# Storing the transposed blocks of x once, in the preparation, and loading them back in layer 1's stage

## The chip, the core and the metric

The kernel runs on one core of a Trainium2 chip. The metric is the device time of one execution in microseconds (us). A core has TensorE (PE in the profile; PEld is its weight load), VectorE (DVE), ScalarE (ACT), GpSimd (POOL) and SyncE (SP, which here only issues transfers). Each engine carries out its own instructions in order; semaphores hold one engine back for another. Transfers run on 16 DMA engines which the queues of SP, ACT and POOL share.

## What is computed

Two layers of a relational graph attention network on 3125 nodes with 768 features and 53125 edges of three relations, then a residual and a layernorm:

```python
xr = jnp.einsum('nd,rdf->rnf', x, W)
oi = xr[etype, dst]; oj = xr[etype, src]
alpha = jax.nn.leaky_relu(oi @ q + oj @ k, NEG_SLOPE)
e = jnp.exp(alpha - segment_max(alpha, dst)[dst])
a = e / (segment_sum(e, dst)[dst] + EPS)
out = segment_sum(a[:, :, None] * oj.reshape(...), dst) + b
...
h = jax.nn.elu(rgat_conv(x, W1, q1, k1, b1, ...))      # 4 heads
out = rgat_conv(h, W2, q2, k2, b2, ...)                # 1 head
return _layernorm(x + out)
```

## The kernel before, in words

Nodes are taken in 25 blocks of 128 rows (the last has 53), features in 6 pieces of 128. Every float32 product is made of three in a reduced form (fp32r): a matrix is split into a high and a low part, and high·high, high·low and low·high are summed. TensorE multiplies along the partitions, so a block of x must be transposed, 6 pieces of 128x128, before it can be multiplied by W. The order of all instructions is written out by hand; nothing is rescheduled. Four stages follow one another.

**The preparation** (to about 120 us). `weights_kq` folds the weights of the queries and keys, `nodes_kq` then makes every node's query and key values. It goes over x two blocks a step, m = 1 to 12, and the single block 0 ahead of them. `Buffers` (`go`, L189) loads x into seven shared tiles, a new block whenever one is freed; one of the seven is lent to the rows of block 0 most of the time, so six turn over. Each `turn(m)` makes 12 transposes (`transposes`, L271) into three PSUM tiles `pt0` to `pt2` with two buffers each, frees the two tiles of x at once, brings the result of two steps ago into place (`place`, L379, L381), and splits the transposed data (`split_parts`: ScalarE copies the high part, L281; VectorE subtracts, L282). Then TensorE does a piece of block 0's own rows (`first`, L403, which ScalarE copies out, L410), and `product(m-1)` (L293), whose result ScalarE copies out of the one PSUM tile `bank` (`sm`, L370) for the next steps. In `weights_kq` L321 is the same kind of copy.

**Layer 1's keys' stage**, `phase1` (about 120 to 655 us): 144 groups of 18 products (`d_group`, L724) make the feature rows of blocks 1 to 24 for three relations, six groups to a block; ScalarE copies each result to one of three row tiles (L743) and SP stores it to the table `tab1` (L745). A list of events by group number n holds all the rest: VectorE's work on edges and softmax, a few small products, and, six groups apart, a block of x: `x_load` brings block b into the tile `xr` (L524), `d_turn(b)` at n = 6b-8 transposes it again (L701) into PSUM `px`, `d_split(b)` at n = 6b-7 splits it to `xT` (L708 on ScalarE, L709 on VectorE), adds the bias b2 to the untransposed block (L711) and stores the sum in `xb_d` (L712), from which the last stage takes its residual. POOL gathers one key vector for each edge by indirect transfers (L479 into `kt`), and every sixth product waits for a certain one of them ("an even load"), so that gathers and products go side by side. W2 is split beside this and, in the last groups, loaded by ScalarE's queue over the parts of wH and wL that are no longer needed (L532).

**Layer 2's features**, `phase2` (to about 1396 us): POOL gathers rows of `tab1` (L479 into `share` and `g`); VectorE makes selection matrices (`selp`, L471); TensorE sums (L978) and multiplies by W2 (L1055). Its first gather waits until all rows of `tab1` are stored. **The last stage** sums layer 2's rows (L1260), adds `xb_d` and normalizes.

Transfers of one queue are carried out in their order. SP's queue holds the loads of x, the row stores, the stores of `xb_d` and the edge data; an instruction of SP that waits holds back all behind it.

Of the kernel before, what the change touches and what calls it, by code (L numbers as in the profile page):

```python
# [8 lines left out]
F32 = mybir.dt.float32  # L9
# [11 lines left out]
P = 128  # L21
# [39 lines left out]
def kernel(  # L61
# [48 lines left out]
    tab2 = dram.tile([(N + P) * R, RW], F32, name="ftab2")  # L110
    kt1 = dram.tile([NP * R, 4], F32, name="kt1")
    xb_d = dram.tile([NP + P, D], F32, name="xb_d")
# [235 lines left out]
    def nodes_kq(buf, pre, work, psum, bank, wk, kqs, wH, wL, qq, more, edges_ready):  # L348
# [7 lines left out]
        def turn(m):  # L356
            b, nb = chunk(m)
            pts = transposes(psum, [buf["x", b + c] for c in range(nb)])
            for c in range(nb):
                buf.free("x", b + c)  # L360
            if m > 1:
                place(m - 2, prod.pop(m - 2))
            return split_parts(work, pts, nb * P, "t" if m else "t0")

# [137 lines left out]
    xs = {}  # L502
# [16 lines left out]
    def x_load(pre, b, to=None):  # L519
        n = min(P, N - b * P)  # L520
        xs[b] = pre.tile([P, D], F32, name="xr", bufs=1) if to is None else to[:, :D]
        if n < P:
            V.memset(xs[b], 0.0)
        nc.sync.dma_start(xs[b][:n], x[b * P:b * P + n, :])  # L524

# [12 lines left out]
    def phase1(pre, work, psum, wH, wL, qq):  # L538
# [7 lines left out]
        st = a_st  # L546
# [143 lines left out]
        xt = {}  # L690
        b2r = share[5][:, :D]
# [3 lines left out]

        def d_turn(b):
            xr = xs.pop(b)
            xt[b] = work.tile([P, 2, DT, P], F32R, **spare.get(b, dict(name="xT", bufs=2)))
            pt = psum.tile([P, 2, 512], F32, name="px", bufs=1)
            for t in range(DT):  # L700
                T.transpose(pt[:, t // 3, (t % 3) * P:(t % 3 + 1) * P], xr[:, t * P:(t + 1) * P], ident)  # L701
            p3 = pt[:, :, :3 * P]
            st["x", b] = xr, p3

        def d_split(b):
# [77 lines left out]
        nc.sync.dma_start(q1_d[NP:, :], als[0].rearrange("p j h -> p (j h)")[:, :H1 * R * 3 // 2].bitcast(BF))  # L783
        d_turn(1)
        d_split(1)
# [18 lines left out]
        GB = NB - 4  # L804
# [17 lines left out]
        for b in range(NB - LATE, NB):  # L822
            n = 6 * b + 2
# [18 lines left out]
        for b in range(2, GB + 1):  # L842
            for d, f, o in ((-8, d_turn, 0), (-7, d_split, 0), (-7, x_next, 1)):
                ev.setdefault(6 * b + d, []).append((f, NB - 1 if f is x_next and b == GB else b + o))
        last_w2 = second_weights(R - 1, wH, wL)
        for n in range(max(ev) + 1):
            for f, b in ev.get(n, ()):
                f(b)
            b, i = divmod(n, 6)
            if n == 2:  # L850
                nc.sync.dma_start(share[3][:, :D], x[:P, :])
            if n == 8:
                V.tensor_add(share[4][:, :D], share[3][:, :D], b2r)
                nc.sync.dma_start(xb_d[:P, :], share[4][:, :D])
            m = n - 6 * (GB - 1)
            if m in (1, 3, 5):
                d_turn(GB + 1 + m // 2)
                d_split(GB + 1 + m // 2)
# [1149 lines left out]
```

## Time and profile before

| what | value |
|---|---|
| three runs | 1985.41, 1987.32, 1988.5 us; median 1987.32 |
| the profiled execution | 1984.63 us, of it 1982.8 us span |
| preparation, layer 1's stage, layer 2's features, last stage (about) | 120, 535, 740, 585 us |
| PE busy over the span | 1680.7 us (85%) |
| POOL, DVE, ACT busy | 1333.2, 1201.9, 376.5 us |
| transposes of the preparation, L271 | 258 |
| transposes of layer 1's stage, L701 | 144 |
| chain that ended last | PE 60%, issue 10%, POOL 8%, DMA 7%, DVE 5% |

The page's chain follows the work that ended last back from the last instruction; its shares say which engine set the end. "Idle before, releaser" is the time that an engine had nothing to do, and what ended it. In a timeline a row is start, duration, engine, line, operation, output<-input and, in brackets, the idle time ahead of it. A row of the windows gives busy time and instruction count of each engine in a stretch, the granted clock of TensorE, the busy share of the DMA engines and GB/s.

### The profile page before, as it was taken

What the parts mean: (1) busy time and instruction counts of PE and PEld (TensorE: products, weight loads), DVE (VectorE), ACT (ScalarE), POOL (GpSimd) and SP (SyncE); (2) the same over time, 40 slices, a digit from 0 to 9 for tenths busy, and PEclk for the clock granted to TensorE, in tenths of its full rate; (3) what the DMA queues carried; (4) which work ended last, traced back from release to release, by engine and by line L of the source; (5) the groups of instructions that cost most, each with busy time, mean ns of one, the idle gap of its engine ahead of it and who ended that gap; (6) DMA issues with size and microseconds to landing.
All of it is one profiled execution on the core that took longest, in us unless ns stands there. A gap on an engine that the chain in (4) does not pass through costs nothing.

```text
span 1982.8 us, 41452 instructions
## 1 busy us (share of the span) xinstructions
PE 1680.7 (85%) x14727; PEld 1406.6 (71%) x14727; DVE 1201.9 (61%) x4296; ACT 376.5 (19%) x661; POOL 1333.2 (67%) x1326
## 2 busy tenths in 40 slices
PE   6989999999999599999999999999465556556664
PEld 6979999999999489898989999899222223223322
DVE  6544555555554667767776777774456665666564
ACT  5421222221221011111111111111011211121111
POOL 4247777777771467777777776652577777777773
PEclk8989999999999899999999999999677777777777
DMA  7556545554557988888888888886799999999994
GB/s 196 191 122 189 179 162 187 170 167 159 182 186 242 365 274 272 294 271 278 272 297 268 276 273 297 271 277 215 252 322 334 331 334 347 335 318 317 327 321 145
DMA packets 161018, 506.48 MB, mean 255 GB/s; under 512 B 47925, under 2 KB 61244, under 8 KB 160803
## 3 DMA queue, kind: packets, MB, share of 16 engines
q0 software_dynamic: 81904, 331.52, 50.6%
q1 hardware_dynamic: 67101, 156.21, 22.3%
q10 hardware_dynamic: 11798, 16.00, 2.5%
q8 instruction: 120, 1.97, 0.4%
q14 instruction: 95, 0.78, 0.1%
HBM read 412.74 MB, written 95.69 MB: 256 GB/s over the span
## 4 chain that ended last, share of the span: by engine, by line
PE 60%; issue 10%; POOL 8%; DMA 7%; DVE 5%; ACT 1%; POOLq 0%; DVEq 0%; ACTq 0%; SPq 0%
PE po L1055 25%; PE po L724 20%; PE acc L978 10%; POOL G L479 8%; DMA G<-ftab,ridx 6%; PE acc L1260 2%; PE pt L1030 1%; DVE selp L471 1%; PE px L701 1%; PE acc L1272 1%; DVE share L674 0%; DVE F L1219 0%; DMA share<-ftab,rfirst 0%; DVE share L675 0%; DVE sT L624 0%
## 5 line engine op out<-in xcount | busy, mean ns | idle before, releaser
L1055 PE MATMUL po<-wH,hT 128*128 128x386 f32 (+1 forms) x1800 | 485.0, 344 | 3.1 <-DVE hT L1043 2.2
L479 POOL DMA_INDIRECT kt<-kt,ridx x374 | 397.4, 1062 | 113.9 <-issue 106.6
L479 POOL DMA_INDIRECT G<-ftab,ridx x374 | 376.2, 1006 | 113.9 <-issue 99.3
L724 PE MATMUL po<-wH,xT 128*128 128x384 f32 x1584 | 435.7, 346 | 5.5 <-ACT share L743 2.4
L471 DVE TENSOR_SCALAR selp<-frow,fdl,pall 128x32 f32<-128x32 f32 (+1 forms) x1688 | 384.0, 321 | 0.7 <-PE acc L978 0.7
L1055 PEld LDWEIGHTS po<-wH,hT 128*128 128x128 f32 x1800 | 330.5, 189 | 18.8 <-issue 14.7
L479 POOL DMA_INDIRECT share<-ftab,ridx x239 | 239.2, 1001 | 100.7 <-PE acc L978 47.4
L1055 PE MATMUL po<-wL,hT 128*128 128x386 f32 (+1 forms) x900 | 305.6, 340 | 0.0
L724 PEld LDWEIGHTS po<-wH,xT 128*128 128x128 f32 x1584 | 292.9, 190 | 9.3 <-ACT share L743 4.2
L724 PE MATMUL po<-wL,xT 128*128 128x384 f32 x792 | 269.5, 340 | 0.0
L1260 PE MATMUL acc<-G,selp 128*32 128x386 f32 x2292 | 249.2, 584 | 6.6 <-DVE selp L471 6.6
L1260 PEld LDWEIGHTS acc<-G,selp 128*32 128x32 f32 x2292 | 126.8, 128 | 102.7 <-issue 53.7
L479 POOL DMA_INDIRECT g<-ftab,ridx x135 | 135.2, 1001 | 64.5 <-PE acc L978 34.0
L978 PE MATMUL acc<-share,selp 128*32 128x193 f32 x3088 | 165.7, 330 | 13.5 <-DVE selp L471 11.1
L1063 ACT COPY r<-po 128x386 f32<-128x386 f32 (+1 forms) x150 | 72.3, 482 | 550.5 <-PE po L1055 550.5
L1055 PEld LDWEIGHTS po<-wL,hT 128*128 128x128 f32 x900 | 170.6, 190 | 0.0
L724 PEld LDWEIGHTS po<-wL,xT 128*128 128x128 f32 x792 | 151.1, 191 | 0.0
L978 PEld LDWEIGHTS acc<-share,selp 128*32 128x32 f32 x3088 | 114.0, 111 | 48.0 <-issue 22.0
L1171 DVE TENSOR_SCALAR sT<-bc,cols 128x512 bf16<-128x512 f32 (+1 forms) x125 | 82.5, 660 | 89.4 <-PE bc L1165 89.4
L743 ACT COPY share<-po 128x384 f32<-128x384 f32 x144 | 68.0, 479 | 298.9 <-PE po L724 278.2
L1165 PE MATMUL bc<-d,one 1*128 1x512 bf16 (+1 forms) x125 | 50.1, 400 | 87.2 <-DVE sT L1171 86.1
L978 PE MATMUL acc<-g,selp 128*32 128x193 f32 x1688 | 102.8, 328 | 1.5 <-DMA g<-ftab,rfirst 1.5
(288 smaller groups left out, 1923.5 us busy)
## 6 DMA issues: line engine op xcount, KB each, us to landing
ftab<-share SPq DMA_DIRECT2D x75, 386.0 KB
ftab<-r SPq DMA_DIRECT2D x75, 386.0 KB
share<-in_L_gnn_W_dram SPq DMA_DIRECT2D x36, 384.0 KB
w_d<-w2hl SPq DMA_DIRECT2D x18, 768.0 KB
sT<-dr_d SPq DMA_DIRECT2D x25, 534.0 KB
share<-in_x_dram SPq DMA_DIRECT2D x27, 384.0 KB
xb_d<-share SPq DMA_DIRECT2D x25, 384.0 KB
xr<-in_x_dram SPq DMA_DIRECT2D x21, 384.0 KB
```

What stands on the lines that cost most here:

```text
L471: V.tensor_scalar(sel.rearrange("p (t f) -> p t f", f=32), of, dl[:, b, j:j + 1], p, op0=ALU.is_equal, op1=ALU.mult)
L479: return G.indirect_dma_start(out=to, out_offset=None, in_=tab, in_offset=_index(i[:, j:j + 1]), bounds_check=NP * R - 1, oob_is_err=False)
L701: T.transpose(pt[:, t // 3, (t % 3) * P:(t % 3 + 1) * P], xr[:, t * P:(t + 1) * P], ident)
L724: m = T.matmul(po[:, :HALF], xT[:, s, t, :], w[:, i, sl], start=(n == 0), stop=(n == 3 * DT - 1))
L743: S.copy(to, po[:, :HALF].rearrange("p (h f) -> p h f", h=2))
L978: T.matmul(acc[32 * t:32 * t + 32, h // 2, c], sel[:, h, 32 * WINDOW[i].index(t):][:, :32], g[:, h * CW:(h + 1) * CW], start=(i == u[0] an ...
L1030: T.transpose(pt[:, t // 3, (t % 3) * P:(t % 3 + 1) * P], s["ey"][:, t * P:(t + 1) * P], ident)
L1055: T.matmul(po[:, :wd], hT[:, k, t, :], w[:, r * DT + t, sl], start=(t == 0 and n == 0), stop=(t == DT - 1 and n == 2))
L1063: S.copy(o[:, c * HW:c * HW + wd], po[:, :wd])
L1165: T.matmul(bc[:, :n], one, s["d"][:, 4 * i * P:4 * i * P + n], start=True, stop=True)
L1171: V.tensor_scalar(s["sT"][:, 4 * i * P:4 * i * P + n], bc[:, :n], cols[:, b:b + 1], None, op0=ALU.is_equal)
L1260: T.matmul(acc[32 * t:32 * t + 32, c, :HW], st[b, j][:, 32 * WINDOW[j].index(t):][:, :32], gs[:, (base(b) + j) % NG, c * HW:(c + 1) * HW], ...
```

## The change

In the preparation, `turn(m)` for m = 1 to 12 now keeps what it has transposed: after the split, the three PSUM tiles are copied back over the two tiles of x they came from (the first block's by ScalarE, the second's by VectorE, three copies of 128x256 each) and stored to a new array `xt_d`, by the queue of ScalarE and that of POOL. Only then are the tiles freed. `place` is moved ahead of the split's copies and the new ones behind.

In layer 1's stage `d_turn` and its PSUM tile are gone. `x_load` takes a block of `xt_d`, already transposed, and `d_split` splits it from SBUF. The sum with b2 gets a load of x of its own: `x_rows` at every n = 6b-3 of block b brings the block into the tile `share[4]` and `x_bias` two groups later adds b2 in place and stores it, from block 0 at n = 0 and 2 up to block 24 at n = 141 and 143. In the kernel before, that store came with `d_split`, for the last block at n = 125.

```diff
@@ nodes_kq: turn
             pts = transposes(psum, [buf["x", b + c] for c in range(nb)])
-            for c in range(nb):
-                buf.free("x", b + c)
             if m > 1:
                 place(m - 2, prod.pop(m - 2))
-            return split_parts(work, pts, nb * P, "t" if m else "t0")
+            parts = split_parts(work, pts, nb * P, "t" if m else "t0")
+            for c in range(nb):
+                if m:
+                    t = buf["x", b + c]
+                    for i, pt in enumerate(pts):
+                        (V.tensor_copy if c else S.copy)(
+                            t[:, 2 * i * P:2 * (i + 1) * P].rearrange("p (f n) -> p f n", f=2),
+                            pt[:, :, c * P:(c + 1) * P])
+                    (G if c else nc.scalar).dma_start(xt_d[(b + c) * P:(b + c + 1) * P, :], t)
+                buf.free("x", b + c)
+            return parts
@@ x_load
-        n = min(P, N - b * P)
         xs[b] = pre.tile([P, D], F32, name="xr", bufs=1) if to is None else to[:, :D]
-        if n < P:
-            V.memset(xs[b], 0.0)
-        nc.sync.dma_start(xs[b][:n], x[b * P:b * P + n, :])
+        nc.sync.dma_start(xs[b], xt_d[b * P:(b + 1) * P, :])
@@ phase1
-        def d_turn(b):
-            xr = xs.pop(b)
-            ...
-            for t in range(DT):
-                T.transpose(pt[:, t // 3, (t % 3) * P:(t % 3 + 1) * P], xr[:, t * P:(t + 1) * P], ident)
         def d_split(b):
-            xr, p3 = st.pop(("x", b))
-            xT = xt[b].rearrange("p s (c t) n -> p s c (t n)", c=2)
-            S.copy(xT[:, 0], p3)
-            V.tensor_sub(xT[:, 1], p3, xT[:, 0].bitcast(F32))
+            raw = xs.pop(b)
+            xt[b] = work.tile([P, 2, DT, P], F32R, **spare.get(b, dict(name="xT", bufs=2)))
+            xT = xt[b].rearrange("p s t n -> p s (t n)")
+            S.copy(xT[:, 0], raw)
+            V.tensor_sub(xT[:, 1], raw, xT[:, 0].bitcast(F32))
+
+        def x_rows(b):
+            n = min(P, N - b * P)
+            if n < P:
+                V.memset(share[4][:, :D], 0.0)
+            nc.sync.dma_start(share[4][:n, :D], x[b * P:b * P + n, :])
+
+        def x_bias(b):
             xb = share[4][:, :D]
-            V.tensor_add(xb, xr, b2r)
+            V.tensor_add(xb, xb, b2r)
             nc.sync.dma_start(xb_d[b * P:(b + 1) * P, :], xb)
@@ the loop over n
-            if n == 2:
-                nc.sync.dma_start(share[3][:, :D], x[:P, :])
-            if n == 8:
-                V.tensor_add(share[4][:, :D], share[3][:, :D], b2r)
-                nc.sync.dma_start(xb_d[:P, :], share[4][:, :D])
+            if n == 0 or n % 6 == 3 and b < NB - 1:
+                x_rows(b + 1 if n else 0)
+            if n == 2 or n % 6 == 5 and b < NB - 1:
+                x_bias(b + 1 if n > 2 else 0)
             if m in (1, 3, 5):
-                d_turn(GB + 1 + m // 2)
                 d_split(GB + 1 + m // 2)
```

The events of `d_turn` are taken out of the list too, and two calls for block 1.

More of the change, by code (lines that the diff above doesn't have):

```diff
@@ L111 @@
     kt1 = dram.tile([NP * R, 4], F32, name="kt1")
+    xt_d = dram.tile([NP, D], F32, name="xt_d")
     xb_d = dram.tile([NP + P, D], F32, name="xb_d")
@@ L694, in phase1, with d_split @@
         spare = {NB - 2: dict(name="kq2", bufs=1), NB - 1: dict(name="w2hl", bufs=1)}
-        def d_turn(b):
-            xr = xs.pop(b)
+        def d_split(b):
+            raw = xs.pop(b)
             xt[b] = work.tile([P, 2, DT, P], F32R, **spare.get(b, dict(name="xT", bufs=2)))
-            pt = psum.tile([P, 2, 512], F32, name="px", bufs=1)
-            for t in range(DT):
[L701 to L705, printed above, removed]
-            xr, p3 = st.pop(("x", b))
-            xT = xt[b].rearrange("p s (c t) n -> p s c (t n)", c=2)
-            S.copy(xT[:, 0], p3)
-            V.tensor_sub(xT[:, 1], p3, xT[:, 0].bitcast(F32))
+            xT = xt[b].rearrange("p s t n -> p s (t n)")
[7 more added lines that the diff above has]
+        def x_bias(b):
             xb = share[4][:, :D]
-            V.tensor_add(xb, xr, b2r)
+            V.tensor_add(xb, xb, b2r)
             nc.sync.dma_start(xb_d[b * P:(b + 1) * P, :], xb)
@@ L783, in phase1 @@
         nc.sync.dma_start(q1_d[NP:, :], als[0].rearrange("p j h -> p (j h)")[:, :H1 * R * 3 // 2].bitcast(BF))
-        d_turn(1)
         d_split(1)
@@ L842, in phase1 @@
         for b in range(2, GB + 1):
-            for d, f, o in ((-8, d_turn, 0), (-7, d_split, 0), (-7, x_next, 1)):
+            for d, f, o in ((-7, d_split, 0), (-7, x_next, 1)):
                 ev.setdefault(6 * b + d, []).append((f, NB - 1 if f is x_next and b == GB else b + o))
```

## The prediction, made blind

> **What bounds the kernel now.** I read the busy time by stretches first (start:end, length, busy us of PE, PEld, DVE, ACT, POOL with instruction counts, granted clock, DMA share, GB/s):
>
> ```profile
> 62.00:104.00 42.00, 41.49 (x311) 38.99 (x309) 21.29 (x54) 19.68 (x48) 10.10 (x29) 1.00 0.53 170
> 122.00:655.00 533.00, 519.00 (x3340) 504.66 (x3341) 273.82 (x825) 104.00 (x205) 377.56 (x352) 0.99 0.57 185
> 655.00:695.00 40.00, 16.65 (x199) 10.64 (x197) 26.19 (x109) 2.63 (x5) 25.26 (x25) 0.78 0.98 357
> 600.00:655.00 55.00, 54.29 (x371) 53.09 (x371) 23.64 (x85) 7.84 (x17) 5.13 (x6) 1.00 0.83 282
> ```
>
> TensorE sets the pace in the preparation and in layer 1's stage; the passage into layer 2's features (655 to 695) is full of transfers instead. Then the timeline of PE, where a block is transposed:
>
> ```profile
> 298.58 0.34 PE L724 MATMUL po<-wH,xT 128*128 128x384 f32 x1
> 298.75 0.82 PE L701 MATMUL px<-fident,xr 128*128 128x128 f32 x6
> 299.33 0.42 PE L724 MATMUL po<-wH,xT 128*128 128x384 f32 x1
> 299.59 0.34 PE L724 MATMUL po<-wL,xT 128*128 128x384 f32 x1
> ```
>
> Products start every 0.175 us. Here two intervals take 1.01 us instead of 0.35: the six transposes cost 0.66 us of TensorE, not their listed 6 x 0.27, since they overlap. At 145.26 to 146.27 it is the same 0.66.
>
> Third, a step of the preparation, by the timelines of PE, ACT and DVE (each step lasts 4.25 us):
>
> ```profile
> 73.91 1.33 PEld L271 LDWEIGHTS pt<-fident,share 128*128 128x128 f32 x12
> ...
> 75.95 1.57 ACT L281 CAST tH<-pt 128x512 fp32r<-128x512 f32 x3
> ...
> 76.57 1.89 DVE L282 TENSOR_TENSOR tL<-pt,tH 128x512 fp32r<-128x512 f32 x3 [0.24 <-ACT tH L281]
> ...
> 78.50 0.37 ACT L370 COPY sm<-bank 48x256 f32<-48x256 f32 x1 [0.98 <-PE bank L293]
> ```
>
> ACT has 0.98 us free ahead of `sm`, which TensorE needs soon after the next transposes. Last, the end of layer 1's stage (SP's and POOL's timelines):
>
> ```profile
> 645.94 9.95 SPq L745 DMA_DIRECT2D ftab<-share  x4
> ```
>
> ```profile
> 662.43 1.00 POOL L479 DMA_INDIRECT share<-ftab,rfirst  x1 [55.78 <-DMA wL<-w_d]
> ```
>
> The last product of the stage starts at 654.7, its row is stored from about 655.5, but the first gather of layer 2's features starts only at 662.43: the store takes 6.5 us among ScalarE's weight loads. (The releaser named is a weight load; the gather's own condition is the rows.)
>
> **What goes.** Transposes of 24 blocks. The first, at 120, bought nothing: the first group's third product waits for the low part on VectorE, which comes at 124.5 behind the edge work (123.25 + 0.42), changed or not. So 23 x 0.66 = **-15.2 us**, TensorE being 97% busy. What is late next? Not POOL: its 354 gathers run from 119.4 to about 607 at 1.38 us, so group 143's gather is 48 us early. The softmax is closer: TensorE waited 11 times, 5.5 us in all, for ACT's exponential (L679). In about a third of the blocks the shorter group lies inside that latency: up to 7 x 0.66; I take **+2** (0 to 4). At the start of the stage the store of `xb_d` (384 KB) no longer stands ahead of the edge data that TensorE waits for at 136.8 (2.76 us), and SP is free 0.5 us earlier: 0.5 + 384 KB at 390 GB/s = **-1.5** (-2.5 to 0).
>
> **What is moved.** The split reads SBUF instead of PSUM: L711, both inputs in SBUF, takes 0.949 us against L709's 0.956, and ACT's L311 from SBUF 0.83 against 0.80: nothing. `x_rows` comes two groups ahead of its add, over 7 us; a weight load of this size at 477.71 was landed by 481.8: VectorE will not wait. But `x_rows` and `x_bias` of block 24 now stand at n = 141 and 143, in SP's queue ahead of the last rows: 53 rows (163 KB) and 393 KB. From 648 to 663 SP's queue moved 0.30, 0.36, 0.39, 0.33 and 0.20 MB in 3 us each, some 0.115 MB per us, behind ScalarE's loads, and it was never empty. 0.556 / 0.115 = 4.8 us later for the last row, for the gather at 662.43, and for all behind it. I take **+4.5** (0, if the queues share otherwise, to 7).
>
> **What is added in the preparation.** No row shows it, so it is bounded from both sides.
>
> *On the engines.* Copies of 256 columns out of PSUM take 0.36 us (t0H, L281); a store's issue 0.37 on ACT (L413), 0.55 to 0.8 on POOL. ACT's step grows from 0.24 + 1.57 + 0.37 = 2.2 us by 3 x 0.36 + 0.4 to 3.7 of 4.25. In the built order each ACT copy waits for VectorE's subtraction on the same PSUM tile, so the copies end at 78.46 + 0.4, and `sm` starts 0.75 us late: just inside its slack, except where a row copy (0.5 us) or its store stand there too. That is about +0.3 in four steps. At m = 1 `sm` of the weights (60.99) goes behind copies, a store, a row copy and its store: +1.1. In the tail it starts at 114.15 instead of 112.68: +1.4. Together **+3.5**, which is the whole price if the transfers cost nothing.
>
> *On the buffers.* Now a tile is free when its transposes end; then, when its store has landed. Six tiles, two a step, so the load must be back three steps later: 12.75 us. The new way round: 4.55 us from the start of the transposes to the end of the subtraction (73.91 to 78.46), 0.75 for the copies, 0.7 for POOL's issue, the store, 0.4 for SP's issue, the load. The first weight load shows one transfer alone: issued at 0.75, used at 4.34, so 3.2 us behind its issue. 6.0 + 3.2 + 0.4 + 3.2 = 12.8: no margin, where before there was 1.4 + 0.4 + 3.2 = 5. And a step then moves 4 x 0.393 MB + 0.07 of rows = 1.64 MB, at the 390 to 400 GB/s that full stretches show 4.2 us, the whole step. So each pair of transfers stands in the other's way: one transfer time (1.0 us) more each for store and load makes 14.8, 2 us late, and that three times (m = 3, 6, 9, 12): **+6**. Ends: 0 (the lag lies in waits counted above), and +13, if each takes 5 us in a full system (6.0 + 0.4 + 10.4 = 16.8, 4 us late, three times, and 1 in the tail).
>
> The Trainium skill, "DMA: Bandwidth & Descriptors", section "Anatomy of one DMA — SWDGE (gpsimd) path", gives a fixed 2.0 us and bytes over 436 GB/s: an estimate of 2.9 us for these, so the way round would take 12.2 us and cost nothing (the fast rival). The same section lays most of the fixed part on the receipt of the write, heaviest from HBM's side, which speaks for the slow one. The row says 3.2 for a load; no store is shown alone.
>
> **Sum.** -15.2 + 2 - 1.5 + 4.5 + 3.5 + 6 = -0.7 us. Against the profiled execution (1984.63: 1982.8 of span and 1.8 around it) 1983.9. The median of the runs shown is 2.7 us above that execution; from it, 1986.6. I forecast **1986.5**. This kernel's runs differ by 3 us, so a change under 0.2% (4 us) can hardly be told from none.
>
> **Rivals.**
>
> 1. *No change worth the name* (forecast), the terms as above: within 4 us. Chance 0.38.
> 2. *The stores are hidden.* The way round stays under 12.75 us, and the last store of `xb_d` slips in beside the weight loads: -15.2 - 1.5 + 3.5, 1 for the softmax and 3 for the end make -9, **1978**. For it: DMA share 0.53 from 62 to 104, and bursts that die down between steps. Against: the traffic doubles just there. Chance 0.28. (This is the rival that the page's formula above gives.)
> 3. *The buffers become the bound.* The preparation runs at the pace of store and load: +13, and the whole is -0.7 + 7 = +6.3, **1993.5**. It decides from a way round of 16.4 us, -6.7 + 3 x (16.4 - 12.8) = +4; below 13.7 us the change gains 4. For it: two stores and two loads in each step fill the engines; SP's queue is served in order, so one late store holds back the next load. Against: from m = 10 on nothing more is loaded. Chance 0.30.
> 4. *TensorE's time is not the bound in layer 1's stage*, and the gain goes into new waits for ACT and for gathers: all but 5 us are lost, +9.5, **1997**. Against: 519 of 533 us busy, gathers early. Chance 0.04.
>
> Range: the ends of the terms reach from -16.7 - 1 + 3.5 + 0 = -14 to -15.2 + 4 + 7 + 3.5 + 13 = +12; without the outer tenth on each side, 1977 to 1997. Faster by over 0.2%: 0.28 (rival 2). Within: 0.38. Slower: 0.34 (3 and 4).
>
> **What would show it.** In the profile after: no L701's px rows, and the start of the last product's group about 14 us closer to the first one's; if not, the first step is wrong. Twelve transposing steps: TensorE waiting there for DMA `share` from m = 5 or 6 on, 2 us at a time, says buffers; evenly 0.3 us for ACT, engines only. First products of layer 1's stage at about 132 instead of 122.8. Between the last product and the first gather 12 us instead of 7.5; if it stays 7.5, the queue was not in the way. The Trainium skill, "PSUM — Partial Sum Buffer", section "PSUM bank collisions raise a hardware error", has two engines kept off one bank; the built order's waits agree, and without them the tail would be about 1 us shorter. It would be all wrong if the loads of `xt_d` held up groups, or if VectorE stood at `x_bias`.

## The result, and the profile after

The changed kernel takes **2009.57 us** (median of 6 runs, 2007.15 to 2012.97) where the kernel before takes 1987.91 beside it (1982.7 to 1989.33): ratio 1.012, 95% interval 1.0108 to 1.0132. It is 21.7 us slower; 1986.5 was forecast, 1977 to 1997 the range. The profiled execution took 2009.1 us, 24.5 more than that of before. Three moments divide it: the first key gather of POOL (the preparation has ended), the start of the last product of layer 1's stage, and the first gather of layer 2's features.

| stretch, us | before | after | difference | forecast |
|---|---|---|---|---|
| to the first key gather | 119.44 | 141.89 | +22.45 | +9.5 |
| from there to the last product | 535.25 | 525.58 | -9.67 | -14.7 |
| from there to layer 2's first gather | 7.74 | 18.08 | +10.34 | +4.5 |
| all the rest | | | +1.4 | 0 |

So all three terms missed to the same side, the preparation by most. The third stretch is called the passage below. The windows of the changed kernel (columns as before: start:end, length, busy time of PE, PEld, DVE, ACT, POOL, granted clock, DMA share, GB/s):

```profile
62.00:104.00 42.00, 34.38 (x240) 31.87 (x241) 22.18 (x61) 20.84 (x56) 10.90 (x26) 0.96 0.76 260
104.00:142.00 38.00, 25.93 (x156) 22.69 (x154) 18.50 (x67) 17.32 (x45) 6.32 (x16) 0.85 0.60 200
144.00:667.00 523.00, 507.03 (x3197) 493.27 (x3198) 272.18 (x823) 102.63 (x204) 381.75 (x353) 0.98 0.64 206
667.00:686.00 19.00, 2.21 (x26) 1.57 (x24) 11.32 (x46) 0.79 (x2) 0.45 (x1) 0.59 0.86 303
```

From 62 to 104 us TensorE is busy 34.4 us instead of 41.5, and the DMA share is 0.76 instead of 0.53. Where it stands is told by the starts of the steps, the transposes in PE's timeline:

```profile
71.40 1.47 PE L272 MATMUL pt<-fident,share 128*128 128x128 f32 x12
79.32 1.70 PE L272 MATMUL pt<-fident,share 128*128 128x128 f32 x12
...
99.10 0.27 PE L272 MATMUL pt<-fident,share 128*128 128x128 f32 x1
101.55 1.42 PE L272 MATMUL pt<-fident,share 128*128 128x128 f32 x11 [2.18 <-DMA share<-in_x_dram]
...
116.60 0.30 PE L272 MATMUL pt<-fident,share 128*128 128x128 f32 x1 [0.81 <-DVE share L367]
119.96 1.91 PE L272 MATMUL pt<-fident,share 128*128 128x128 f32 x11 [3.05 <-DMA share<-in_x_dram]
125.64 0.27 PE L272 MATMUL pt<-fident,share 128*128 128x128 f32 x1
128.76 1.42 PE L272 MATMUL pt<-fident,share 128*128 128x128 f32 x11 [2.85 <-DMA share<-in_x_dram]
```

A step that mostly took 4.25 us takes 4.2 to 9. The bracket names the cause where TensorE itself waits: a block of x has not landed, from step 8 on. Of the 16.3 us by which steps 1 to 12 grew, 9.5 lie from step 8 on. Step 3 to step 4 (71.40 to 79.32), 3.7 us longer than before, is another matter: ScalarE's copy of block 0's row waited 2.45 us for a store (`DMA xt_d<-share`), since the tile lent to that row was one that had just been stored, and `sm` stood behind it. After a wait TensorE can be slower: 11 transposes took 1.91 us behind the wait of 3.05 us, instead of 1.42, and the granted clock from 120 to 124 us was 0.59.

In layer 1's stage the trace shows a wait that the forecast had excluded. From VectorE's waits between 144 and 680 us (total in us, times, longest):

```profile
DVE share L717 <- DMA share<-in_x_dram: 66.1, 17, 12.3
```

L717 is the sum with b2: VectorE stood 17 times, 66 us. And the passage at its end, SP's and POOL's timelines:

```profile
659.73 0.30 SPq L713 DMA_DIRECT2D share<-in_x_dram  x1
660.13 2.22 SPq L751 DMA_DIRECT2D ftab<-share  x2
675.46 0.34 SPq L718 DMA_DIRECT2D xb_d<-share  x1
676.25 1.08 SPq L751 DMA_DIRECT2D ftab<-share  x2
```

```profile
685.55 0.99 POOL L488 DMA_INDIRECT share<-ftab,rfirst  x1 [52.53 <-DMA fbias<-in_L_gnn_b_dram]
```

The load of block 24's 53 rows is issued at 659.73, and its sum can be stored only at 675.46. SP issues in order, so the last two row stores stand behind that until 676.25, with the gather behind these. (The load of the bias that the gather's row names is not its condition: in the kernel with the 53 rows split, below, it is issued only after that gather, at 673.67.) From its issue to the sum (674.47) the load of 163 KB took 14.7 us.

### The profile page after: what moved, and what is told of

It is laid out like the page before. It is cut to its first block, busy times and chain, and to the rows that moved or that the text cites. A ratio compares the mean times of both kernels' runs of the same rounds, so it can differ in the third digit from the quotient of the medians.

```text
span 2007.3 us, 41356 instructions
## 1 busy us (share of the span) xinstructions
PE 1676.3 (84%) x14583; PEld 1400.1 (70%) x14583; DVE 1213.7 (60%) x4332; ACT 388.8 (19%) x697; POOL 1344.2 (67%) x1338
## 5 line engine op out<-in xcount | busy, mean ns | idle before, releaser
L1058 PEld LDWEIGHTS po<-wH,hT 128*128 128x128 f32 x1800 | 330.7, 189 | 18.6 <-issue 14.7
```

The source lines that it names most:

```text
L1058: T.matmul(po[:, :wd], hT[:, k, t, :], w[:, r * DT + t, sl], start=(t == 0 and n == 0), stop=(t == DT - 1 and n == 2))
```

## The experiments

In each row below the four stretches come from one profile, so they scatter: three kernels with the same preparation (changed, preparation alone, x + b2 early) give 69.3, 71.5 and 72.0 us for steps 1 to 12. The moment at which step 1 starts scatters too, 55.7 to 60.8, so the preparation is measured from there. Steps 1 to 12 run from the start of the first transposes of step 1 to those of step 12, the tail from there to the first key gather. The stage is counted from that gather to the start of its last product, the passage from there to layer 2's first gather. The expectations of the first kernels, down to x plus b2 early, count it from the products that wait for edge data, 17.4 us later (518 us before, 508 changed). Each ratio is to runs of the kernel before made beside that kernel, whose medians lie between 1986.21 and 1988.27. Four kernels (stage alone, copies without stores, stores without copies, half-width stores) leave out the transposition of what the stage splits: they give prices and are no solutions.

| kernel | median us | ratio (95%) | steps 1-12 | tail | stage | passage |
|---|---|---|---|---|---|---|
| before | | 1 | 52.98 | 10.59 | 535.25 | 7.74 |
| changed | 2009.57 | 1.012 (1.011-1.013) | 69.30 | 16.25 | 525.58 | 18.08 |
| preparation alone | 2013.75 | 1.014 (1.012-1.017) | 71.54 | 15.50 | 533.12 | 7.66 |
| stage alone | 1986.05 | 0.999 (0.998-1.000) | 52.97 | 10.76 | 526.26 | 17.84 |
| copies, no stores | 1991.87 | 1.002 (1.001-1.004) | 54.28 | 14.62 | 522.92 | 17.74 |
| stores, no copies | 2017.48 | 1.015 (1.013-1.017) | 64.47 | 25.30 | 527.96 | 17.70 |
| two tiles of their own | 2010.71 | 1.012 (1.010-1.013) | 74.08 | 14.44 | 523.53 | 18.30 |
| x + b2 early | 1997.01 | 1.005 (1.004-1.007) | 72.00 | 15.35 | 519.75 | 7.77 |
| both of these | 1995.59 | 1.004 (1.003-1.006) | 73.79 | 16.59 | 521.03 | 7.64 |
| eight tiles | 2011.73 | 1.012 (1.010-1.014) | 60.66 | 24.56 | 525.25 | 18.14 |
| 53 rows split | 1998.64 | 1.006 (1.004-1.008) | 69.54 | 11.87 | 523.01 | 9.64 |
| four tiles, split | 1988.75 | 1.001 (1.000-1.002) | 61.99 | 13.08 | 525.39 | 9.08 |
| half-width stores, split | 1988.02 | 1.000 (0.999-1.001) | 58.45 | 12.57 | 529.46 | 10.01 |
| late blocks, split | 1988.48 | 1.001 (1.000-1.002) | 53.13 | 14.44 | 531.87 | 7.95 |
| four tiles, split, early | 1982.38 | 0.998 (0.997-0.999) | 58.67 | 13.06 | 523.74 | 7.68 |
| eight tiles, split | 1995.75 | 1.004 (1.003-1.006) | 62.17 | 12.80 | 525.73 | 9.77 |
| eight tiles, split, early | 1990.69 | 1.001 (1.000-1.002) | 64.52 | 13.94 | 521.24 | 7.50 |

### The two halves of the change

The kernel before with the new `turn(m)` alone:

```diff
-            return split_parts(work, pts, nb * P, "t" if m else "t0")
+            parts = split_parts(work, pts, nb * P, "t" if m else "t0")
...
```

> The kernel before, with the copies and the stores of the transposed blocks added in its preparation, and nothing else: layer 1's stage still loads x, transposes it and makes x plus b2 as before (what is stored is read by nobody). Theory (the two halves of the change have separate prices): the preparation alone costs what it cost in the whole change, so the first gather of layer 1's stage at 142 us instead of 119.4 (140 to 143.5), that stage as long as before from there to its last product (518 us), the passage into layer 2's features 7.5 us, and the time about 2010 (2007 to 2012). Rival (part of the 22 us comes from something else, such as the loads of stored blocks that the stage makes at its start): first gather at 136 or before and a time under 2004.

The changed kernel with `turn(m)` as before:

```diff
-        nc.sync.dma_start(xs[b], xt_d[b * P:(b + 1) * P, :])
+        nc.sync.dma_start(xs[b][:n], x[b * P:b * P + n, :])
```

> The changed kernel without the copies and stores in the preparation; its layer 1 stage splits rows of x as they lie, without any transposition (this leaves the transposition out: the keys' tables of blocks 1 to 24 are those of other numbers, with the same instructions and bytes). Theory: first gather at 119.5 us, the stage from there to its last product 508 us (506 to 511) instead of 518, the passage into layer 2's features 18 us (16 to 19) instead of 7.5, and the time 1988 (1985 to 1991): the gain of the transposes is given back at once at the end. Rival (the long passage is an after-effect of the late start, with other queues shifted against each other): passage under 12 us, time about 1980.

Measured: the first gather comes at 145.77 and 119.46 us, the passage takes 7.66 and 17.84. So the halves have separate prices: the preparation costs as much alone as in the whole change, and the long passage belongs to the stage's half, however early that starts. (The preparation alone was dearer than expected, with a gather 2.3 us past the range and 2013.75 us where 2012 was its end. Its step 1 started 2.4 us later than the changed kernel's; from there to the gather it takes 87.0 us and the changed kernel 85.6.) With the stage alone, the stage gains 9.0 us and gives them back in the passage.

### Engines or transfers

```diff
-                    (G if c else nc.scalar).dma_start(xt_d[(b + c) * P:(b + c + 1) * P, :], t)
```

> The changed kernel with the copies in the preparation but without their 24 stores; the stage loads rows of x as they lie (the transposition of what it splits is left out, as in the run of the stage alone). So this is the price of the engines' copies without the transfers. Theory (transfers and the buffers that wait for them make most of the 22 us): first gather at 123 to 126 us, no wait of TensorE for the x tiles over 1 us. Rival (the copies on ScalarE and VectorE make most of it, through late sm and late place): first gather at 135 us or later.

```diff
-                    for i, pt in enumerate(pts):
-                        (V.tensor_copy if c else S.copy)(...)
+                    (V.tensor_copy if c else S.copy)(t[:, :1], pts[-1][:, 0, c * P:c * P + 1])
```

> The changed kernel with one column copied per block in place of all 768, so that the store still waits for the transposes and holds the tile, but ScalarE and VectorE have almost no copying to do (what is stored is x as it lies, but for one column: the transposition is left out). So this is the price of the transfers and of the tiles that wait for them, with 4 us less engine work in each step. Theory (transfers and buffers): first gather at 132 to 140 us, with waits of TensorE for the x tiles of 2 to 9 us as in the changed kernel. Rival (engines): first gather at 122 us or before. If both runs stay well under their share (the two add up to far less than 22 us), the price is in their joint effect: the copies lengthen the way round that the transfers fill.

Measured: with the copies alone the first gather comes at 125.66, 6.2 late; steps 1 to 12 are only 1.3 us longer. In its tail stands one wait:

```profile
111.04 0.27 PE L271 MATMUL pt<-fident,share 128*128 128x128 f32 x1
113.87 1.42 PE L271 MATMUL pt<-fident,share 128*128 128x128 f32 x11 [2.56 <-DMA share<-in_x_dram]
```

That is block 24 not landed, 2.6 of the 6.2; a wait over the 1 us expected, which was not understood yet. The stores alone cost more than the whole change (148.57), beyond the range expected for them: transfers it is, but 10.6 us of the 29 are again one wait for block 24. With less work for the engines it was dearer, which neither theory had foreseen.

### Tiles

```diff
-                    t = buf["x", b + c]
+                    t = pre.tile([P, D], F32, name="xr", bufs=1) if c else share[6][:, :D]
...
```

with `buf.free` right after the transposes, as before.

> The changed kernel, but the transposed blocks are copied into two tiles of their own, so that a tile of x is free at the end of its transposes, as before the change; copies, stores and their bytes are the same (the small tile of the edge work moves beside another one to make room; block 1 is loaded for layer 1 into that other tile). Theory (the stores cost because the x tiles wait for them, and the loads stand behind those waits in SyncE's queue): the price of the engines' copies remains, 6 us, so the first gather of layer 1's stage at 126 us (125 to 130) instead of 142, waits of TensorE for x tiles under 3 us, time 1994 (1992 to 1998). Rival (bandwidth: stores and loads together are more than the transfers carry in a step): first gather at 135 us or later, time over 2002.

```diff
-            self.spare = list(range(6)) + [7]
+            self.spare = list(range(8))
...
```

> The changed kernel with one more tile for the blocks of x and W in the preparation, eight instead of seven, and nothing else (the small tile of the edge work moves beside another one). Theory (a way round of the tiles that is some 2 us longer than the steps allow, repeated): half a step, 2.1 us, more slack in each way round takes off most waits for x: first gather at 130 us (127 to 134), time 1998 (1995 to 2002). Rival (bandwidth, or the order of the queue): the waits stay, first gather at 138 us or later, time over 2005.

In both the theory's numbers failed and the rivals' came out: 2010.71 and 2011.73, nothing gained, first gathers at 146.16 and 145.58. But the profiles do not show the rivals' causes. With two tiles of their own TensorE no longer waits for x at all; now the copies wait for the stores. ScalarE's store and its next copy, then VectorE's copies around one of POOL's stores (issued at 114.84) and around a late one (135.87):

```profile
79.49 0.33 ACTq L372 DMA_DIRECT2D xt_d<-share  x1
...
85.05 0.92 ACT L369 COPY share<-pt 128x256 f32<-128x256 f32 x3 [2.62 <-DMA xt_d<-share]
```

```profile
123.12 1.09 DVE L369 COPY xr<-pt 128x256 f32<-128x256 f32 x3 [5.08 <-DMA xt_d<-xr]
...
138.60 1.09 DVE L369 COPY xr<-pt 128x256 f32<-128x256 f32 x3 [0.20 <-DMA xt_d<-xr]
```

The bracket ends where the store has landed, so a store takes 5.6 us (79.49 to 85.05) and 8.3 us (114.84 to 123.12) beside loads, and 2.7 us (135.87 to 138.60) when no load runs. Of the nine stores of this trace that a copy waited for, seven took 4.0 to 8.3 us; the last two, with no load of x beside them, took 3.1 and 2.7. Beside loads that is mostly more than a step (4.25 us), so one tile for each half of a step is not enough: the wait had only moved. With eight tiles, steps 1 to 12 did become 8.6 us shorter, and the tail ate it:

```profile
121.02 0.27 PE L272 MATMUL pt<-fident,share 128*128 128x128 f32 x1
132.24 2.61 PE L272 MATMUL pt<-fident,share 128*128 128x128 f32 x11 [10.95 <-DMA share<-in_x_dram]
```

Block 24 once more, now 10.95 us.

### x plus b2 early

```diff
-            if n == 0 or n % 6 == 3 and b < NB - 1:
-                x_rows(b + 1 if n else 0)
-            if n == 2 or n % 6 == 5 and b < NB - 1:
-                x_bias(b + 1 if n > 2 else 0)
+            if n % 5 == 0 and n // 5 < NB:
+                x_rows(n // 5)
+            if n % 5 == 3 and n // 5 < NB:
+                x_bias(n // 5)
```

> The changed kernel with x plus b2 made ahead of its due time: a block every 5 groups instead of 6, the sum three groups after the load instead of two, so that the last block is stored at group 123 of 144 rather than at 143. Theory (the long passage is the load and store of x plus b2 ahead of the last rows in SyncE's queue, and VectorE's stand at the sum costs the stage 2 to 4 us): passage from the last product to the first gather of layer 2's features 7.5 to 10 us instead of 17.9, VectorE's wait for these loads under 20 us instead of 66, stage 504 to 507 us instead of 508, time 1997 (1994 to 2001). Rival (the rows wait for the weights that ScalarE loads, whatever stands ahead): passage over 15 us, time over 2004.

Together with the two tiles of their own:

> Both edits together, the tiles of their own in the preparation and x plus b2 early. Theory: the prices add, 6 us in the preparation, about -11 in the stage, 1 at the end, so 1983 (1980 to 1987), a little faster than the kernel before. Rival (bandwidth in the preparation, or the weights at the end): 1992 or more.

Measured: 1997.01, as expected. The passage is 7.77, as before the change, the stage 519.75 (501.3 by the expectation's measure, shorter than its 504 to 507), and VectorE's wait has shrunk to

```profile
DVE share L717 <- DMA share<-in_x_dram: 1.9, 1, 1.9
```

What this load took is read from SP's issue and the end of VectorE's wait in the changed kernel: 341.45 to 348.73 and 361.62 to 368.25, so 7.3 and 6.6 us, against a lead of about 7 us that VectorE, running ahead of its turn, used up. In four pairs that differ by this edit (changed, two tiles, four tiles split, eight tiles split) the stage is 5.8, 2.5, 1.7 and 4.5 us shorter with it. Some of that may be scatter: the ten profiles of the table whose stage is the changed kernel's but for this edit give 522.9 to 529.5 us, 525.5 in the mean, the four with it 519.8 to 523.7, 521.4 in the mean. So about 4 us, with an uncertainty of some 2. The version with both edits missed its 1980 to 1987 and came out in the rival's range (1995.59): its preparation is as dear as the one with two tiles alone.

### Bytes, and a chip with a lower clock

Four tiles of their own, two of them taken out of the seven in step 1:

```diff
-                    t = buf["x", b + c]
+                    t = buf["stage", c] if m % 2 == 0 else (
+                        pre.tile([P, D], F32, name="xr", bufs=1) if c else share[6][:, :D])
...
```

> The changed kernel with four tiles of their own for the transposed blocks, two for each block of a step in turn, so that a store has two steps (8.5 us) to land before a copy waits for it; tiles of x are free at the end of their transposes, and two of the seven become such tiles in step 1, so that x has five. In the run with two such tiles the stores landed 5.6 to 8.3 us after their issue while loads ran beside them (2.7 to 3.1 in the tail, alone) and the copies waited for them. Theory A (the price is the stores' landing time, and any tile that waits for it hands it on): with two steps to land nothing waits, first gather at 126 to 131 us, time 1992 to 1999. Theory B (loads and stores together are more bytes than a step carries, so the wait goes from tile to tile, now back to the loads): TensorE waits for x again, first gather at 136 us or later, time 2003 or more.

```diff
-  xt_d[(b + c) * P:(b + c + 1) * P, :], t)
+  xt_d[(b + c) * P:(b + c + 1) * P, :HALF], t[:, :HALF])
...
```

> The changed kernel with all copies and all 24 stores, but each store takes only the first 384 of the 768 columns, 192 KB in place of 384; the stage loads rows of x as they lie (the transposition of what it splits is left out). Theory A (a store's fixed latency): stores still hold their tiles some 5 us, first gather at 137 us or later. Theory B (bytes): a step moves 1.25 MB in place of 1.64, which fits into it at 340 GB/s (3.7 us of 4.25), so first gather at 126 to 131 us, near the 125.7 of the copies without stores.

The kernel before, with `turn(m)` changed for m >= 9 alone and x plus b2 of these blocks in `share[6]`:

```diff
...
+    STORED = 17
...
-        nc.sync.dma_start(xs[b][:n], x[b * P:b * P + n, :])
+        nc.sync.dma_start(xs[b][:n], (xt_d if b >= STORED else x)[b * P:b * P + n, :])
...
+            if n % 12 == 2 and STORED + n // 12 < NB:
+                x_rows(STORED + n // 12)
+            if n % 12 == 8 and STORED + n // 12 < NB:
+                x_bias(STORED + n // 12)
```

> The kernel before, with the change for blocks 17 to 24 alone (steps 9 to 12 of the preparation, in which nothing or little is loaded any more); blocks 1 to 16 are transposed in layer 1's stage as before. x plus b2 of the eight stored blocks is made between groups 2 and 92, in a tile that is free then, six groups after its load. Theory B (the price is loads and stores beside each other): the stores cost nothing here, the copies 1 to 3 us; the stage gains 8 x 0.66 = 5.3 less some latency; the passage stays 7.5; first gather at 121 to 123 us, time 1984 (1981 to 1987). Rival (the stores' latency or their place in the queues costs wherever they stand): first gather at 126 us or later, time 1990 or more.

These three ran on a chip that granted a clock of 0.81 to 0.82 in the mean, where the kernel before takes 2657.13 us; their times are 2652.66, 2651.55 and 2628.89 (ratios 1.000, 1.000 and 0.992, interval 0.989 to 0.995) and are not compared with the others. But from 60 to 100 us their clock was 0.96 to 1.00, as in the other runs, and the wait for block 24 was there again in all three, 9.8, 8.5 and 10.3 us. So their first gathers, at 144.40, 139.15 and 136.74, all fall where theory B for the four tiles, theory A for the half width and the rival for the late blocks had them, and decide little, since that wait is in each of them. The version with the late blocks isolates it:

```profile
111.65 0.27 PE L272 MATMUL pt<-fident,share 128*128 128x128 f32 x1
122.25 2.61 PE L272 MATMUL pt<-fident,share 128*128 128x128 f32 x11 [10.33 <-DMA share<-in_x_dram]
```

SP issued block 24's load at 107.48 us and others after it; it landed at 122, nearly 15 us later. From 115 to 120 us PE, DVE and ACT did nothing at all and the DMA share was 0.34.

### Fifty-three rows

The queues' own rows then gave the cause (q1 is SP's queue, q10 ScalarE's; packets, MB, share of the 16 engines). First the kernel *before*, from 104 to 106 us, when SP's queue holds little but this load, then the passage of the changed kernel, SP's queue from 666 to 669 us and both from 672 to 675:

```profile
q1 hardware_dynamic: 16, 0.05, 6.2%
```

```profile
q1 hardware_dynamic: 122, 0.33, 27.6%
...
q10 hardware_dynamic: 637, 0.95, 94.1%
q1 hardware_dynamic: 15, 0.04, 4.1%
```

6.2% of 16 engines is what one engine makes that is never idle. It carries a packet of 3 KB in 0.125 us (16 in 2 us) when it is free, and in 0.2 us (15 in 3 us) when ScalarE's loads share it: 53 rows in 7 to 11 us, plus what stands ahead. The Trainium skill has the rule for it, in "DMA: Bandwidth & Descriptors", section "Why a DMA increments its semaphore by 16 and not by 1": a transfer uses the largest number of engines up to 16 that divides its outermost dimension. 53 is a prime, so that is one; the trace agrees (6.2%).

The other rows of the passage set something right that stands ahead of the prediction, that transfers of one queue are carried out in their order: SP issues them in order, but the 0.33 MB from 666 to 669 us are mostly the two row stores issued after the load of 53 rows (660.13), and that load was not used before 674.47.

The busy engine holds up stores as well. In the kernel with two tiles of their own, the load of 53 rows was issued at 114.92, beside the store of 114.84 that took 8.3 us. From 122 to 124 us the queues of SP, ScalarE and POOL took 2.8%, 2.6% and 0.9% of the 16 engines, together 6.3%, so one engine: the ends of the stores took turns there with that load.

In the next kernel both loads of the 53 rows are made in two parts, of 48 rows and of 5:

```diff
+            k = n // 16 * 16
-            nc.sync.dma_start(share[4][:n, :D], x[b * P:b * P + n, :])
+            nc.sync.dma_start(share[4][:k, :D], x[b * P:b * P + k, :])
+            if k < n:
+                nc.sync.dma_start(share[4][k:n, :D], x[b * P + k:b * P + n, :])
...
```

That is `x_rows`; `go` has the same, for the preparation. The same two edits are then put on the four tiles, the half-width stores and the late blocks of above:

> The changed kernel with the loads of block 24's 53 rows, in the preparation and for x plus b2, each made as one of 48 rows and one of 5. Theory C (a load of 53 rows is served by one of the 16 DMA engines, so its 159 KB take 10 to 15 us where a full block takes 3 to 5; in the passage it trickled at 15 packets of 3 KB in 3 us beside ScalarE's loads): the wait for block 24 at the last transposes goes, first gather at 136 to 140 us instead of 142 to 146; VectorE's sum no longer stands 12 us, and the passage is what the forecast's queue made it, 11 to 13 us instead of 17.9; time 2000 (1996 to 2003). Rival (the queue is long for all transfers there, whatever their shape): the passage stays over 16 us, first gather at 141 or later, time over 2006.

> Four tiles of their own for the transposed blocks, and the loads of 53 rows in two parts. Theory A (stores' landing time, which nothing waits for with two steps to land) plus C: first gather at 126 to 130 us, passage 11 to 13, time 1988 to 1993. Theory B (loads and stores are more bytes than a step carries) plus C: TensorE still waits for x from step 8 on, first gather at 133 us or later, time 1995 or more.

> All copies, stores of 384 of the 768 columns (the stage loads rows of x as they lie, so the transposition of what it splits is left out), and the loads of 53 rows in two parts. Theory B plus C: half the bytes, about half the price of the transfers; first gather at 128 to 132 us, between the 125.7 without stores and the 136 to 140 with whole ones. Theory A (latency): first gather as with whole stores, 136 or later.

> The kernel before with the change for blocks 17 to 24 alone, as in the earlier run of that kind, and the loads of 53 rows in two parts. In that run the first transposes of block 24 waited 10.3 us for its load, which had been issued behind the store that freed its tile, 4 us before. Theory C: with the load on all engines that wait is under 1 us, first gather at 121 to 123 us, stage 4 to 5 us shorter than before, passage 7.5: time 1984 (1981 to 1987). Rival (the late load waits for the stores beside it): first gather at 126 us or later, time 1988 or more.

Measured: the split alone takes 11 us off, 1998.64, with the first gather at 140.36, 0.4 past its range. The transposes of the last step go through in one, and in the passage the sum's store and the gather come 7.3 and 17.4 us after the load's issue instead of 15.7 and 25.8:

```profile
128.49 1.48 PE L275 MATMUL pt<-fident,share 128*128 128x128 f32 x12
```

```profile
655.64 0.35 SPq L717 DMA_DIRECT2D share<-in_x_dram  x1
656.04 0.35 SPq L719 DMA_DIRECT2D share<-in_x_dram  x1
...
662.95 0.34 SPq L724 DMA_DIRECT2D xb_d<-share  x1
```

```profile
673.01 1.05 POOL L491 DMA_INDIRECT share<-ftab,rfirst  x1 [40.06 <-DMA wL<-w_d]
```

The passage is 9.64, shorter than the 11 to 13 expected. (Two parts whose rows do not divide so well, such as 47 and 6, were not tried.) With this cause gone the others can be told apart. What is left of the way round shows in SP's queue, here from 50 to 135 us (total in us, times, longest):

```profile
SPq L191 <- DMA xt_d<-share: 51.0, 15, 8.7
```

L191 is the load of a block of x, which waits until the store from its tile has landed. With four tiles of their own no load of x waits for such a store any more. Four tiles take 7.5 us off steps 1 to 12 (61.99 against 69.54), half the bytes 11.1 (58.45); the copies alone had 54.28. The gathers at 132.64 and 129.07 lie between the two theories for the four tiles, where TensorE still waits once, 3.0 us, for a block of x, and inside the one of bytes for the half width. Both hold in part: tiles wait for stores, and the stores are slow by what runs beside them. The late blocks have no such wait any more (steps 1 to 12 at 53.13), but it did not pay either: 1988.48 where 1984 was expected, and a first gather at 124.51, past its 121 to 123, since the tail is 3.9 us longer and the stage only 3.4 shorter.

### All together

The edits are those shown: four tiles, split loads and x plus b2 early; then eight tiles with split loads, without and with x plus b2 early.

> All three edits to the changed kernel that took something off its price: four tiles of their own for the transposed blocks, the loads of 53 rows in two parts, and x plus b2 made early (a block every 5 groups, the sum three groups after the load). Theory (the prices are separate): the preparation costs what it did with four tiles and split loads, first gather at 132 to 134 us (13 us late); the stage from first gather to last product is as with x plus b2 early, 520 us against 535 before (-15); the passage is 7.5 us: sum -2, time 1985 (1982 to 1988) beside 1987 to 1988 of the kernel before. Rival (VectorE's stand at x plus b2 was hidden, and the shorter stage of that run came from its late start): stage 525 us, time 1990 or more.

> The changed kernel with eight tiles in place of seven, and the loads of 53 rows in two parts. With eight tiles alone, steps 2 to 12 took 49.8 us (before 43.3, changed 58.5, changed with split loads 58.7), but then block 24 was waited for 10.9 us. Theory (the tiles' way round is most of the price between steps 2 and 12, and the load of 53 rows hid what an eighth tile gains): steps 2 to 12 in 48 to 51 us, no long wait for block 24, first gather at 130 to 134 us, time 1989 to 1993. Rival (bytes: the wait comes back elsewhere): steps 2 to 12 in 55 us or more, first gather at 137 or later, time 1996 or more.

> The same with x plus b2 made early (a block every 5 groups). Theory: 2 to 5 us less in the stage and 2 in the passage than with eight tiles and split loads, so 1984 to 1988, about as the kernel before and within 3 us of the version with four tiles of their own. Rival (bytes in the preparation): 1990 or more.

Measured: four tiles, split loads and x plus b2 early make **1982.38** us against 1986.21 for the kernel before, ratio 0.9981, interval 0.997 to 0.9991: the one complete version here that is faster than both kernels, by 0.2%. Its first key gather, last product and first gather of layer 2's features:

```profile
129.32 1.10 POOL L496 DMA_INDIRECT kt<-kt,rfirst  x1 [5.84 <-DVE n_all L602]
...
660.74 1.02 POOL L496 DMA_INDIRECT share<-ftab,rfirst  x1 [39.25 <-DMA wL<-w_d]
```

The preparation costs 9.9 us by the gather (8.2 from the start of step 1), the stage gains 11.5, the passage nothing: -1.7, and the span is 2.2 us shorter. The stage's 523.74 lies nearer to the rival's 525 than to the 520 expected, while the preparation came out better (129.32 for 132 to 134). Here the transfers are full: from 75 to 120 us the DMA share is 0.96, at 330 GB/s, where the changed kernel has 0.83. A step's 1.64 MB would take 5.0 us at that rate (an estimate), and a step has 4.25. Eight tiles with split loads miss their ranges by a little (steps 2 to 12 in 51.3 us, gather at 134.74, time 1995.75) though no long wait is left, so the way round is most of the price there, and not all; with x plus b2 early as well they are level with the kernel before (1990.69, 1.0008, interval 0.9996 to 1.0019), above the range expected and in the rival's; step 1 started late there (60.79), as in all three with eight tiles, and why was not tried.

## Why the prediction was wrong

**The transposes** went as forecast, within the scatter. The pace of layer 1's stage was TensorE's, and without VectorE's stand the stage is 11.5 to 15.5 us shorter than before (523.74, 521.24, 521.03, 519.75), for 14.7 forecast; measured against the preparation alone, which has the stage of before at 533.12, it is 9.4 to 13.4. Rival 4 (TensorE not the bound) is refuted. The 1.5 us at the stage's start did not come: from the first gather to the products that wait for edge data it is 17.4 us in both.

**"VectorE will not wait" at `x_bias`** failed. The load was taken from one row of another load, 4.1 us; behind row stores in the same queue those of full blocks that VectorE waited for took 3.8 to 8.9, and VectorE is early. The price is some 4 us of the stage, 1.7 to 5.8 in the four pairs; with the 1.5 us at the start it makes the difference between -14.7 and -9.67.

**The end** was right in its place and its queue, and wrong in the cause of most of it. The forecast priced block 24's load as 163 KB at 0.115 MB per us, 1.4 us; it took 14.7. Of the 10.3 us, 8.4 go with the split (18.08 to 9.64) and 1.9 stay, for the 4.5 forecast and 0 as its lower end. The row that shows it was in the trace of before, a trickle of one engine from 104 to 106 us; there it cost nothing, since the block was needed only at 109 us, 11 after the load's issue.

**The engines' copies** in the preparation were forecast at 3.5. Copies alone measured 6.2, of it 2.6 the wait for block 24, so 3.7 remain. The 1.4 forecast for the tail's late `sm` fit the changed kernel with split loads, whose tail is 1.3 us longer than before (11.87 against 10.59); the other kernels with split loads have 2.0 to 3.9, which was not explained. (The listed parts of this term add up to 3.7, not 3.5.)

**The buffers** were the step that failed most: +6 was forecast with 0 and +13 as ends, and some 15 came, with 4.4 us more from a load that the sum put at nothing. From the start of step 1 the preparation is 22.0 us longer. The copies take 2.8 of this by the same measure, the load of 53 rows 4.4 (the tail, 16.25 to 11.87), and 15 are left for the way round. The way round was the right mechanism, and rival 3 came true in its mechanism though not in its time (1993.5), as its terms were too small: a store was put at 3.2 us and one transfer time more, 5 at the worst, and took 4.0 to 6.5 beside whole loads and up to 8.3 beside the load of 53 rows. And a step's bytes were reckoned at 390 to 400 GB/s, 4.2 us; with stores and loads mixed, the full stretch of the last experiments moved 330. The Trainium skill's formula that the forecast weighed ("DMA: Bandwidth & Descriptors", section "Anatomy of one DMA — SWDGE (gpsimd) path", 2.9 us by it) fits a store alone, 2.7 to 3.1, and not one among loads; so the fast rival that rested on it fell. It was also not seen that the lent row tile and the load of the last block hang on the same stores. Four tiles take 6 to 10 of the 15 away, half the bytes 10. How the rest divides between full transfers and single waits was not settled.

## What to carry to other kernels

Work that is moved to a stage with idle engines still needs that stage's transfers and tiles: count the way round of a tile with the landing time of a store among loads, read from a stretch as full as the new one will be, not from a transfer alone. A wait that moves when a buffer is added has not been explained; look for what stands behind it before believing that the bytes are the bound. And look at the odd last block: a shape that costs nothing behind slack becomes the end of the chain once that slack is used.

## What the runs showed of the hardware

A load of 53 rows of 3 KB kept one DMA engine busy (6.2% of 16). Where something waited for it, it was used 9 to 17 us after its issue in the preparation and 14.7 in the passage; made of 48 and 5 rows, 6.3 in the passage. Stores of 384 KB landed in 2.7 to 3.1 us without loads of x, in 4.0 to 6.5 beside whole ones and in up to 8.3 beside the load of 53 rows (two tiles of their own). After waits of 8 to 11 us TensorE made 11 transposes in 2.61 us instead of 1.42, in five kernels: a stall costs more than its length. And on the chip with the lower clock the kernel with the late blocks was 0.8% faster than the one before, where its version with split loads made no difference on another chip; that transposes weigh more where TensorE is slower would explain it, but was not tried.
